# First FFN of a graph network in three parts: two early parts of 16 and 12 blocks beside the first attention, the rest behind it

## The chip, the cores and the metric

The kernel runs as one program on one core of a Trainium2 chip. The metric is the time of one execution on the device in microseconds (us); the median of ten executions is what is compared.

## The reference

6250 nodes with 256 features pass through four residual layers: graph attention, a routed FFN with eight experts, a weighted neighbour sum, and a second FFN whose experts are chosen by another graph attention. Both graphs' edges come with the inputs. What the change touches is the second layer, which needs the first:

```python
x = x + _L0_gnn_ref(_layernorm(x, axis=-1), edge_index, ...)      # graph attention, 206250 edges, 4 heads
x = x + _L0_ffn_ref(_layernorm(x, axis=-1)[None], ...)[0]         # routed FFN, below
x = x + _L1_gnn_ref(_layernorm(x, axis=-1), src, dst, edge_weight, ...)
x = x + _L1_ffn_ref(_layernorm(x, axis=-1)[None], ...)[0]

def _L0_ffn_ref(x, Wr, br, ln_g, ln_b, W1, b1, W2, b2):           # D = 256, E = 8 experts, H = 1024
    logits = xt @ Wr + br
    top_p, top_idx = jax.lax.top_k(jax.nn.softmax(logits), 2)
    weights = top_p / top_p.sum(axis=-1, keepdims=True)
    xn = layer norm of xt over its features
    xe = xn[None] * ln_g[:, None] + ln_b[:, None]
    h = jax.nn.gelu(jnp.einsum('end,edh->enh', xe, W1) + b1[:, None], approximate=False)
    y = jnp.einsum('enh,ehd->end', h, W2) + b2[:, None]
    out = (weights[:, :, None] * the two chosen rows of y).sum(axis=1)
```

A node's row of the FFN depends on its own row of the attention's output alone, so blocks of nodes can go through the FFN as soon as they are through the attention.

## The kernel before

The nodes, padded to 6272, are 49 blocks of 128. The edges, sorted by target, are 1612 tiles of 128, and 8 tiles (`Q`) make a piece; there are 202 pieces.

**First attention.** `gat_stream` (from L1497) runs one step per piece, in an order written out by hand (`manual_schedule`, L1722): instructions stand on each engine's queue in program order. Step `s_` has POOL issue 8 gathers of source rows (L1582, one for each tile), computes scores of the piece gathered one step earlier on VectorE, and adds the messages of the piece gathered seven steps earlier into PSUM on TensorE (L1691). The gathered rows have nine buffers. When a block's sums are complete, `done`, `normed`, `twice` and `logits` follow it, one of them per step, and write its normalized rows to a table in DRAM (L2223 for early blocks, L2225 for the others). `ends` (L2239) says after which blocks the two experts of a group of blocks are chosen; for early blocks a group has four blocks at most.

**The early part.** The first `EARLY` = 22 blocks belong to one `EarlyPart`. For each of its groups, a step apart: `chosen` (three parts of the ranking per step), `counted` (ranks inside the group, two matmuls, L789 and L790), `ranked` (places), and `put` (each block is loaded back from its table and scattered to its two experts' regions by POOL, L823). Behind the last group `tiles_of` (L833) turns the eight counts into a table of tiles of 256 rows, with two iotas on POOL; `filled` (L870) has SP read eight counts and write zeros behind each region (L876), and finds each token's place in the result and its gates. Then the part is `ready`.

The part's `beside` is a generator. The stream's steps call it five times each, and two of five calls return at once (L2251), so three slots a step remain. First come the expert parameters and the lists of the second graph, one after the other; then it waits for `ready` and goes into `run` (L898): after a start of four slots, every tile takes nine slots, with the tile's weights (`w`, three buffers of 1 MB, L922 and L927), its rows (L920) and its result (L983) on SP's queue, the first matmul at L953, the gelu at L959 and the second matmul at L975. `self.tiles` is the number of tiles that any routing could need, so the count doesn't depend on the data. When the stream's steps are over, whatever is left of the generator runs without them (L1790).

**The rest.** `head.ffn` calls `routed_ffn` (L494) for the other 27 blocks once the attention is complete. It ranks them on VectorE, finds the places with `2 * NT` small matmuls (L588), and runs tiles of 256 rows (`run_tiles`, L597): gathers of rows by POOL (L612), matmuls at L636 and L649, scatters of results (L652). `TT` tiles are the most that a routing can need; the last `n_exp // 2` = 4 of them stand behind a condition on the device (`more`, L548, and L674). After each tile it calls the generator `beside` `calls` times; with it comes `first.combined` (L988), which for each early block gathers the two results (L995), adds them to the block (L1008), and writes it and its normalized form to DRAM. The chunks of seven blocks at the end (L679) do the same for the rest.

```python
self.tiles = (2 * n * P + E0 * (TS - 1)) // TS           # L763, TS = 256, E0 = 8
TT = (2 * NP + n_exp * (TS - 1)) // TS                   # L505
TM = TT - n_exp // 2                                     # L514
nc.vector.tensor_scalar(more, end[:, n_exp - 1:], float(TM) + 0.5, None, op0=OP.is_gt)
```

The weighted sum (`weighted_sum`, L2288) reads the tables that both write, and starts behind them.

Of the kernel before, what the change touches and what calls it, by code (L numbers as in the profile page):

```python
# [20 lines left out]
F32 = mybir.dt.float32  # L21
BF = mybir.dt.bfloat16
I32 = mybir.dt.int32
I16 = mybir.dt.int16
AF = mybir.ActivationFunctionType
OP = mybir.AluOpType
# [6 lines left out]
P = 128  # L33
# [38 lines left out]
def tile_kernel(ctx, tc, src_ins, out):  # L72
    nc = tc.nc
# [680 lines left out]

    EARLY = 22

    class EarlyPart:


        def __init__(self, pool, head, n):  # L760
            TS = 2 * P
            self.head, self.n = head, n
            self.tiles = (2 * n * P + E0 * (TS - 1)) // TS  # L763
            self.cap = n * P + TS
            self.tab_x = dram.tile([n * P, D], F32, name="tab_xa")
            self.by_expert = dram.tile([E0 * self.cap, D], F32, name="xa_e")
            self.tab_y = dram.tile([self.tiles * TS, D], F32, name="tab_ya")
            self.inc = pool.tile([P, n, E0], F32, name="inca")
            self.g2 = pool.tile([P, n, 2], F32, name="g2a")
            self.place = pool.tile([P, 2, n], I32, name="placea")  # L770
            self.where = pool.tile([P, 2, self.tiles], I32, name="wherea")
            self.ready = False

        def begin(self, pool, ps):
            self.pool, self.ps = pool, ps
            self.count = pool.tile([P, E0], F32, name="counta")
            nc.vector.memset(self.count, 0.0)
            self.eo = pool.tile([P, E0], F32, name="eoa")
            nc.gpsimd.iota(self.eo, pattern=[[self.cap, E0]], base=0, channel_multiplier=0,
                           allow_small_or_imprecise_dtypes=True)  # L780
            self.zero = pool.tile([P, D], F32, name="zeroa")
            nc.vector.memset(self.zero, 0.0)

        def counted(self, t0, n, mp):
            sel, inc = self.head.sel[:, t0:t0 + n], self.inc[:, t0:t0 + n]
            nc.vector.tensor_copy(inc[:, 0], sel[:, 0])
            for t in range(1, n):
                nc.vector.tensor_add(inc[:, t], inc[:, t - 1], sel[:, t])
            nc.tensor.matmul(self.ps[:, 0], before, inc[:, n - 1], start=True, stop=True)  # L789
            nc.tensor.matmul(self.ps[:, 1], ones, inc[:, n - 1], start=True, stop=True)  # L790
            return self.ranked, (t0, n, mp)

        def places(self, dst, ranks_, start, n, mp):
            sel = self.head.sel[:, ranks_:ranks_ + n]
            r = mp.tile([P, n, E0], F32, name=f"rka{n}", bufs=1)
# [19 lines left out]
        def put(self, t0, n, mp, pi, j, xs):  # L815
# [4 lines left out]
            if len(xs) == 2 or j == n:  # L820
                i, x = xs.pop(0)
                for k in range(2):
                    st = nc.gpsimd.indirect_dma_start(  # L823
                        out=self.by_expert, out_offset=bass.IndirectOffsetOnAxis(ap=pi[:, k, i:i + 1], axis=0),
                        in_=x, in_offset=None, bounds_check=E0 * self.cap - 1, oob_is_err=False)
                    tc.declare_no_dep(st.ins, group="xa_e", reason="each token has two places of its own")
                    tc.add_to_no_dep_group("xa_e", st.ins)
            if j < n:
# [4 lines left out]
        def tiles_of(self, mp):  # L833
# [13 lines left out]
            nc.vector.tensor_add(zo, self.eo, self.count)  # L847
            tio = p.tile([P, TA], F32, name="tioa")
            nc.gpsimd.iota(tio, pattern=[[1, TA]], base=0, channel_multiplier=0, allow_small_or_imprecise_dtypes=True)
# [5 lines left out]
            wide = [P, TA, E0]  # L855
            w = p.tile(wide, F32, name="wa")
            nc.vector.tensor_tensor(w[:, :, :E0 - 1], tio[:, :, None].to_broadcast([P, TA, E0 - 1]),
                                    end[:, None, :E0 - 1].to_broadcast([P, TA, E0 - 1]), op=OP.is_ge)
            tb = p.tile([P, TA], F32, name="tbb")
            nc.vector.tensor_reduce(tb, w[:, :, :E0 - 1], AX.X, OP.add)  # L860
# [9 lines left out]
        def filled(self, mp, zo, base):  # L870
# [7 lines left out]
            r, pl = self.places(self.place, 0, base, n, self.pool)  # L878
            eq = self.pool.tile([P, n, E0], F32, name="eqa")
            for k in range(2):  # L880
                nc.vector.tensor_tensor(eq, r, pl[:, k, :, None].to_broadcast([P, n, E0]), op=OP.is_equal)
                nc.vector.tensor_mul(eq, eq, self.head.gates[:, :n])
                nc.vector.tensor_reduce(self.g2[:, :, k], eq, AX.X, OP.add)
            self.ready = True

        def beside(self, par, lists):
            for _ in par:
                yield True
            for part in lists:
                with tc.tile_pool(name="srt", bufs=1) as sp, tc.tile_pool(name="srt_ps", bufs=1, space=PSUM) as pp:  # L890
                    for _ in part(sp, pp):
                        yield True
            while not self.ready:
                yield True
            with tc.tile_pool(name="ffa", bufs=1) as fp, tc.tile_pool(name="ffa_ps", bufs=2, space=PSUM) as pp:
                yield from self.run(fp, pp)
# [90 lines left out]

        def combined(self, pool, x_d, x_e, tab_e):  # L988
            def load(b):
                x = pool.tile([P, 1, D], F32, name="xa")  # L990
                nc.sync.dma_start(x[:, 0], x_d[b * P:(b + 1) * P])
                ys = []
                for k in range(2):
                    y = pool.tile([P, D], F32, name=f"ya{k}")
                    nc.gpsimd.indirect_dma_start(  # L995
                        out=y, out_offset=None, in_=self.tab_y,
                        in_offset=bass.IndirectOffsetOnAxis(ap=self.place[:, k, b:b + 1], axis=0))
                    ys.append(y)
                return x, ys

            ahead = load(0)
            yield
            for b in range(self.n):
                x, ys = ahead
                if b + 1 < self.n:
                    ahead = load(b + 1)
                for k in range(2):
                    nc.vector.scalar_tensor_tensor(x[:, 0], ys[k], self.g2[:, b, k:k + 1], x[:, 0], op0=OP.mult, op1=OP.add)  # L1008
                nc.sync.dma_start(x_e[b * P:(b + 1) * P], x[:, 0])
                em = pool.tile([P, 1, D], F32, name="ema")  # L1010
                layernorm(pool, em, x, 1)
                nc.sync.dma_start(tab_e[b * P:(b + 1) * P], em[:, 0])
                yield

# [1124 lines left out]
    def fast(flag_s0, tab, NI, si, dl, il):  # L2139
# [18 lines left out]
        f0 = chosen_by.enter_context(tc.tile_pool(name="f0f", bufs=1))  # L2158
        NA = EARLY
        head = Head(f0, NA)  # L2160
        first = EarlyPart(f0, head, NA)
        with tc.tile_pool(name="gat0f", bufs=1) as g0:
# [57 lines left out]
            def logits(b, mp, xt, mv, sd, xT):  # L2220
                scaled(mp, xt, xt, mv, sd)
                if b < NA:
                    nc.sync.dma_start(first.tab_x[b * P:(b + 1) * P], xt)  # L2223
                else:
                    nc.sync.dma_start(head.tab_x[(b - NA) * P:(b + 1 - NA) * P], xt)  # L2225
                head.logits(mix[:, P + D:P + D + E0], xT, b)
                if b in ends:
                    t0 = max([e + 1 for e in ends if e < b], default=0)
                    n = b + 1 - t0
                    return chosen, (head.select(hp, t0, n), (t0, n) if b < NA else None, mp)  # L2230

            def chosen(parts, early_, mp):
# [3 lines left out]
                if early_ is not None:  # L2236
                    return first.counted, (*early_, mp)

            ends = tuple(min(NA, t + 4) - 1 for t in range(0, NA, 4)) + (NA + (NT - NA) // 2, NT - 6, NT - 1)  # L2239
            with tc.tile_pool(name="f0h", bufs=1) as hp, tc.tile_pool(name="mix_ps", bufs=1, space=PSUM) as xp:  # L2240
                mix = xp.tile([P, 4 * P], F32, name="mix")
                o = P + D + E0
                first.begin(hp, mix[:, o:o + 2 * E0].rearrange("p (k e) -> p k e", k=2))
                par = head.params(hp)
                side = first.beside(par, (lambda sp, pp: sorted_edges(s1, sp, pp, si1, dst1),
                                          lambda sp, pp: weights_of(s0, sp, pp, wt_d),
                                          lambda sp, pp: sorted_ends(s1, sp, pp, dst1, dl1, il1, flag1)))
                turn = itertools.count()

                def beside(flush=False):  # L2250
                    if not flush and next(turn) % 5 in (1, 3):  # L2251
                        return True
                    return next(side, None) is not None

# [27 lines left out]
        with tc.tile_pool(name="early", bufs=2) as yp:  # L2282
            head.ffn(f0, first.combined(yp, x_d, x_e, tab_e), combine, NA, calls=1)
        chosen_by.close()
# [310 lines left out]
```

## Time and profile before

| | us |
|---|---|
| median of 10 runs (6117.49 to 6136.03) | 6126.25 |
| profiled execution, its own time | 6122.44 |
| span of the profiled execution | 6120.7 |
| mean granted TensorE clock | 0.834 |
| first attention: first and last gather (L1582) | 122.6 and 2286.9 |
| lists of the second graph written (last L1935) | 1011.7 |
| early FFN: first and last start at L953 and L975 | 1404.2 and 2303.3 |
| rest of the FFN: first and last start at L636 and L649 | 2407.2 and 2929.3 |
| first gather of the weighted sum (L234) | 2988.2 |

The profile is of one execution. PE is TensorE's matmuls, PEld its weight loads, DVE VectorE, ACT ScalarE, POOL GpSimd, SP the queue that issues most transfers. A slice of the page is a fortieth of the span, 153 us, and a digit a tenth. In a timeline each row has its start and its duration in us, and in brackets the idle time before it and what ended it. The busy time of PE, DVE, ACT and POOL over the span is 4342.9, 3223.1, 1366.1 and 4100.7 us. A matmul of 32-bit floats shows as two records for each instruction, so a tile of the FFN has 32 records in each of its two layers.

### The profile page before, as it was taken

To read this page: it belongs to the slowest core of one execution; us is meant where nothing else is said; L and a number is where in the kernel's file an instruction comes from. 1 tells how busy PE (TensorE), PEld (TensorE's weight loads), DVE (VectorE), ACT (ScalarE), POOL (GpSimd) and SP (SyncE) were. 2 spreads that over 40 slices of the span, in tenths; PEclk is the share of its full clock that TensorE was granted. 3 is DMA by queue.
4 is the path that set the end of the run, shared out by engine and by line. 5 is a ranking of instruction groups with operands and counts; after the bars stand their busy time and mean duration, and the time that the engine had idled before them with its cause. 6 is when DMAs were issued, how large, how long until landed. Compare 5 with 4: busy or idle time off the path is not lost.

```text
span 6120.7 us, 67115 instructions
## 1 busy us (share of the span) xinstructions
PE 4342.9 (71%) x20648; PEld 3312.9 (54%) x20648; DVE 3223.1 (53%) x8690; ACT 1366.1 (22%) x3038; POOL 4100.7 (67%) x4311
## 2 busy tenths in 40 slices
PE   4466666658998997999478899999999997111111
PEld 3344544447777886787245666666666665111111
DVE  5788987656666675311422222222232224777777
ACT  2122111113333342422002222222222223000001
POOL 1777777777777771422377777777777757777774
PEclk8778777779999997999688999999999998555555
DMA  7545465547777774754534444444444433333332
GB/s 186 148 139 145 139 173 170 148 140 240 228 230 222 238 219 147 243 191 156 184 111 120 128 128 127 128 127 129 127 130 129 124 103 93 80 75 78 71 78 51
DMA packets 543876, 890.85 MB, mean 146 GB/s; under 512 B 146208, under 2 KB 384942, under 8 KB 543470
## 3 DMA queue, kind: packets, MB, share of 16 engines
q0 software_dynamic: 190688, 461.74, 28.2%
q1 hardware_dynamic: 333242, 406.39, 20.9%
q10 hardware_dynamic: 19572, 18.23, 0.9%
q8 instruction: 173, 2.83, 0.2%
q14 instruction: 201, 1.65, 0.1%
HBM read 784.77 MB, written 104.42 MB: 145 GB/s over the span
## 4 chain that ended last, share of the span: by engine, by line
PE 27%; POOL 10%; DVE 9%; issue 8%; DMA 5%; ACT 2%; DVEq 0%; SPq 0%; POOLq 0%; ACTq 0%
PE acc L2318 8%; POOL g L234 6%; PE pf L2028 5%; PE pf L2016 5%; POOL g L1582 4%; PE py L649 2%; DMA g<-tab_1f,si1s 2%; PE ph L636 2%; DMA g<-tab_ef,si 2%; PE pf L2026 2%; DVE xo L2116 1%; DVE oh L1458 1%; PE bacc L2334 1%; DVE s L1673 1%; DVE g L1675 1%
## 5 line engine op out<-in xcount | busy, mean ns | idle before, releaser
L1582 POOL DMA_INDIRECT g<-tab,si x1612 | 1578.6, 979 | 538.1 <-issue 490.3
L234 POOL DMA_INDIRECT g<-tab_ef,si x1612 | 1532.5, 951 | 547.4 <-issue 461.9
L2318 PE MATMUL acc<-g,oh 128*128 128x256 f32 x3224 | 867.1, 409 | 213.5 <-DMA g<-tab_ef,si 117.0
L1691 PE MATMUL acc<-g,oh 128*128 128x264 f32 x3224 | 913.7, 440 | 65.4 <-DVE g L1668 54.9
L1582 POOL DMA_INDIRECT g<-tab_1f,si1s x787 | 756.3, 961 | 245.5 <-issue 212.4
L2318 PEld LDWEIGHTS acc<-g,oh 128*128 128x128 f32 x3224 | 614.9, 201 | 451.6 <-issue 268.2
L1691 PEld LDWEIGHTS acc<-g,oh 128*128 128x128 f32 x3224 | 708.4, 223 | 223.8 <-DVE g L1668 70.7
L1668 DVE TENSOR_TENSOR g<-g,mix 128x2048 f32<-128x2048 f32 x202 | 459.6, 2275 | 59.7 <-ACT xT L2217 31.3
L2306 DVE TENSOR_SCALAR oh<-iota,dl,wt 128x128 f32<-128x128 f32 x1612 | 432.1, 362 | 87.8 <-PE acc L2318 83.9
L2016 PE MATMUL pf<-xt,w 128*128 128x512 f32 (+1 forms) x832 | 397.5, 610 | 55.1 <-ACT h L2021 55.1
L1603 PEld LDWEIGHTS <-ot 128*128 128x128 bf16 x2879 | 121.0, 101 | 509.0 <-issue 484.7
L2028 PE MATMUL pf<-w,h 128*128 128x256 f32 x1568 | 394.4, 395 | 0.0
L1691 PE MATMUL acc<-s,oh 128*128 128x72 bf16 x1267 | 91.1, 248 | 369.4 <-DVE s L1673 369.4
L2028 PEld LDWEIGHTS pf<-w,h 128*128 128x128 f32 x1568 | 283.9, 191 | 96.9 <-issue 65.7
L1691 PEld LDWEIGHTS <-oh 128*128 128x128 bf16 x1267 | 85.1, 131 | 377.3 <-issue 366.8
L953 PE MATMUL pf<-xe,w 128*128 128x256 f32 x928 | 231.6, 400 | 54.2 <-DVE xe L946 43.1
L2016 PEld LDWEIGHTS pf<-xt,w 128*128 128x128 f32 x832 | 158.1, 203 | 197.4 <-issue 118.8
L636 PE MATMUL ph<-xe,w 128*128 128x256 f32 x1088 | 248.6, 387 | 13.0 <-ACT h L639 13.0
L1458 DVE TENSOR_TENSOR oh<-zt,dl 128x1024 f32<-128x1024 f32 x202 | 244.5, 1211 | 0.0
L649 PE MATMUL py<-w,h 128*128 128x256 f32 x1088 | 243.8, 382 | 0.0
L636 PEld LDWEIGHTS ph<-xe,w 128*128 128x128 f32 x1088 | 210.7, 194 | 44.7 <-ACT h L639 15.3
L2376 DVE TENSOR_SCALAR ss<-ss 128x1 f32<-128x1 f32 x49 | 7.5, 154 | 418.1 <-ACT ss L2372 418.1
(548 smaller groups left out, 6424.6 us busy)
## 6 DMA issues: line engine op xcount, KB each, us to landing
w<-in_L_ffn_W SPq DMA_DIRECT2D x126, 1024.0 KB
db<-s_d SPq DMA_DIRECT2D x149, 512.0 KB
yb<-y_d SPq DMA_DIRECT2D x49, 640.0 KB
g<-tab,si POOLq DMA_INDIRECT x1612
g<-tab_ef,si POOLq DMA_INDIRECT x1612
y_d<-y SPq DMA_DIRECT2D x196, 128.0 KB
g<-tab_1f,si1s POOLq DMA_INDIRECT x787
bb<-in_L_ffn_b SPq DMA_DIRECT2D x63, 128.0 KB
```

The lines of the kernel that those rows point to most:

```text
L234: nc.gpsimd.indirect_dma_start(out=dst, out_offset=None, in_=table, in_offset=bass.IndirectOffsetOnAxis(ap=si[:, t:t + 1], axis=0))
L636: nc.tensor.matmul(ph, w1[:, k, f * P:(f + 1) * P], xe[:, k, :], start=(k == 0), stop=(k == KD - 1))
L649: nc.tensor.matmul(py, hs[f][:, i * P:(i + 1) * P], w2[:, f, :], start=(f == 0), stop=(f == FC - 1))
L953: nc.tensor.matmul(ph[:, f], w1[:, k, (f0_ + f) * P:(f0_ + f + 1) * P], xe[:, k], start=(k == 0), stop=(k == KD - 1))
L1458: nc.vector.tensor_tensor(o[:, :m], ips[:, None, k * P:(k + 1) * P].to_broadcast([P, m, P]), dl[:, a:a + m, None].to_broadcast([P, m, P]), ...
L1582: nc.gpsimd.indirect_dma_start(out=g[:, j, :DH + H], out_offset=None, in_=tab, in_offset=bass.IndirectOffsetOnAxis(ap=si[:, t0 + j:t0 + j ...
L1668: nc.vector.tensor_mul(gh, gh, ps[0][:, o:o + n, :, None].to_broadcast([P, n, H, CD]))
L1691: nc.tensor.matmul(acc[b].rearrange("p s w -> p (s w)"), oh[:, t - a], m_, start=(t == lo), stop=(t == hi))
L2016: nc.tensor.matmul(ph[:, :n], w1[:, e, k, f * P:(f + 1) * P], xts[g][:, k, :n], start=(k == 0), stop=(k == KD - 1))
L2028: nc.tensor.matmul(py[:, :D], hs[g, e, f][:, j * P:(j + 1) * P], w2[:, e, f, :], start=False, stop=(f == FC - 1))
L2306: nc.vector.tensor_scalar(oh[:, j], iota, dl[:, t0 + j:t0 + j + 1], wt[:, t0 + j:t0 + j + 1], op0=OP.is_equal, op1=OP.mult)
L2318: nc.tensor.matmul(acc[i], oh[:, t - t0], g[:, t - t0, :], start=(t == lo), stop=(t == hi))
```

## The change

`EARLY` becomes `(16, 12)`: two objects of `EarlyPart`, for blocks 0 to 15 and 16 to 27, each with tables, counts and tiles of its own. The ranking groups are those of each part (four blocks at most). The generator beside the stream runs parameters and lists as before, then part 1's tiles when part 1 is ready, then part 2's when part 2 is. The rest has 21 blocks. `combined` becomes one function that goes through the blocks of both parts, and `head.ffn` is asked for two calls of it after each tile. The two parts share the zeros that are written behind the regions, and some scratch tiles.

```diff
-    EARLY = 22
+    EARLY = (16, 12)
...
-        def __init__(self, pool, head, n):
+        def __init__(self, pool, head, t0, n):
             TS = 2 * P
-            self.head, self.n = head, n
+            self.head, self.t0, self.n, self.tag = head, t0, n, f"a{t0}"
             self.tiles = (2 * n * P + E0 * (TS - 1)) // TS
...
-        def beside(self, par, lists):
-            for _ in par:
-                yield True
-            for part in lists:
-                with tc.tile_pool(name="srt", bufs=1) as sp, tc.tile_pool(name="srt_ps", bufs=1, space=PSUM) as pp:
-                    for _ in part(sp, pp):
-                        yield True
+        def beside(self):
             while not self.ready:
                 yield True
-            with tc.tile_pool(name="ffa", bufs=1) as fp, tc.tile_pool(name="ffa_ps", bufs=2, space=PSUM) as pp:
+            with tc.tile_pool(name=f"ff{self.tag}", bufs=1) as fp, \
+                    tc.tile_pool(name=f"ff{self.tag}_ps", bufs=2, space=PSUM) as pp:
                 yield from self.run(fp, pp)
...
+    def combined(early, pool, x_d, x_e, tab_e):
+        todo = [(part, b) for part in early for b in range(part.n)]
+        ahead = todo[0][0].load(pool, x_d, 0)
+        yield
+        for i, (part, b) in enumerate(todo):
+            x, ys = ahead
+            if i + 1 < len(todo):
+                ahead = todo[i + 1][0].load(pool, x_d, todo[i + 1][1])
+            for k in range(2):
+                nc.vector.scalar_tensor_tensor(x[:, 0], ys[k], part.g2[:, b, k:k + 1], x[:, 0], op0=OP.mult, op1=OP.add)
...
-        NA = EARLY
+        NA = sum(EARLY)
         head = Head(f0, NA)
-        first = EarlyPart(f0, head, NA)
+        parts = [EarlyPart(f0, head, sum(EARLY[:i]), n) for i, n in enumerate(EARLY)]
+        part_of = [part for part in parts for _ in range(part.n)]
...
-            ends = tuple(min(NA, t + 4) - 1 for t in range(0, NA, 4)) + (NA + (NT - NA) // 2, NT - 6, NT - 1)
+            ends = tuple(part.t0 + min(part.n, t + 4) - 1 for part in parts for t in range(0, part.n, 4)) + (NA + (NT - NA) // 2, NT - 6, NT - 1)
...
+                def in_turn():
+                    yield from par
+                    for make in lists:
+                        with tc.tile_pool(name="srt", bufs=1) as sp, tc.tile_pool(name="srt_ps", bufs=1, space=PSUM) as pp:
+                            yield from make(sp, pp)
+                    for part in parts:
+                        yield from part.beside()
+
+                side = in_turn()
...
-            head.ffn(f0, first.combined(yp, x_d, x_e, tab_e), combine, NA, calls=1)
+            head.ffn(f0, combined(parts, yp, x_d, x_e, tab_e), combine, NA, calls=2)
```

## The prediction

> **What bounds the kernel now.** I read the slices of the page first, then busy time by stretch, then the queues of single engines where two stages meet. The slices show four stages: lists and first attention (up to slice 14), the rest of the first FFN (to 19), weighted sums, second attention. Only the first two are touched.
>
> ```profile
> PE   4466666658998997999478899999999997111111
> POOL 1777777777777771422377777777777757777774
> PEclk8778777779999997999688999999999998555555
> ```
>
> Slices 7 and 8 (1071 to 1377 us) have a half-idle TensorE. The stretches put numbers to it (columns: length, then busy time of PE, PEld, DVE, ACT, POOL with counts, granted clock, DMA share, GB/s):
>
> ```profile
> 1160.00:1397.00 237.00, 136.73 (x582) 104.44 (x581) 145.83 (x367) 34.91 (x88) 180.15 (x190) 0.76 0.52 148
> 1397.00:2303.50 906.50, 838.63 (x4459) 712.10 (x4458) 603.26 (x1190) 332.01 (x680) 651.56 (x680) 0.98 0.74 228
> 2303.50:2351.20 47.70, 33.24 (x142) 25.80 (x140) 38.39 (x85) 13.01 (x32) 0.00 (x0) 0.91 0.32 107
> ```
>
> Before 1397 nothing is near full by busy time, yet POOL is the bound, as its own timeline shows:
>
> ```profile
> 1105.29 0.94 POOL L1582 DMA_INDIRECT g<-tab,si  x1 [0.30 <-DMA g<-tab,si]
> 1106.54 0.95 POOL L1582 DMA_INDIRECT g<-tab,si  x1 [0.30 <-issue]
> 1107.79 1.02 POOL L823 DMA_INDIRECT xa_e<-xsa,pia  x1 [0.30 <-issue]
> 1109.11 1.01 POOL L823 DMA_INDIRECT xa_e<-xsa,pia  x1 [0.30 <-issue]
> ```
>
> A gather starts every 1.25 us, a scatter of the early part takes 1.32: the 0.30 between them is issue, never a wait. A step of the stream (8 gathers) cannot take under 10.0 us. From 1397 the early FFN runs beside it; 88 steps take 906.5 us, 10.30 each, with PE 93% and POOL (651.6 + 680 x 0.30) / 906.5 = 94% occupied. Two nearly full engines: FFN work beside the stream was almost free, and no room is left there. The FFN alone is PE-bound:
>
> ```profile
> 2784.98 7.07 PE L636 MATMUL ph<-xe,w 128*128 128x256 f32 x32
> 2791.89 0.60 PE L621 MATMUL pt<-ident,xg 128*128 128x128 f32 x4
> 2792.32 7.07 PE L649 MATMUL py<-w,h 128*128 128x256 f32 x32
> 2799.23 7.07 PE L636 MATMUL ph<-xe,w 128*128 128x256 f32 x32
> ```
>
> From L636 to L636 a tile takes 14.25 us.
>
> **How many tiles, and when.** The early part runs (2·n·128 + 8·255)//256 tiles: 29 for 22 blocks; 23 and 19 for 16 and 12, so 42. The rest has 34 before (L636 x1088, 32 records each); for 21 blocks 28, of which the last 4 stand behind a condition (needed > 24). The reference's routing on its own inputs gives blocks 28 to 48 (padding included) 670, 622, 755, 630, 872, 598, 543 and 686 rows per expert, 3+3+3+3+4+3+3+3 = 25 tiles, so the condition holds and all 28 run. In all 63 tiles become 70.
>
> Of five calls of beside per step the code skips two, and a tile has nine yields: 3 steps a tile, as the trace has it (906.5/29 = 31.3 us). Part 1 is ready when block 15 is: the scatters of blocks 12 to 15 end at 1122.8 (start 1121.80), and before, the last scatter (1359.67) came 37 us ahead of the first FFN load (1396.69). So part 1 starts near 1159, 237 us earlier, 22 steps of the loop (counted through its windows, step 92 in place of 114). Part 2's last block, 27, is ready 12 steps after its logits at step 129, long before part 1 ends. 23·9+4 and 19·9+4 slots are 128.7 steps: FFN from step 92 to 220. The last gather is issued in step 201, before's FFN ends in step 202, the loop in step 224. So 22 steps take 7 tiles in free PE time, 29 stand as before, and **6 tiles fall behind the last gather**, where nothing but the end of the stream covers them.
>
> **The sum**, against the profiled execution (6122.4 us, 6120.7 of it span; 3.9 under the median of 6126.25, so I add the change to the median).
>
> 1. Gathers. 24 scatters of blocks 16 to 27 now lie beside FFN (before, 12 of blocks 16 to 21 lay in POOL-bound steps without it). Steps 92 to 102: 11 x 10.30 = 113; 103 to 141: POOL 39 x 10.0 + 24 x 1.32 = 422; together 535 against 237 + 28 x 10.30 = 525 before: **+9**. Bounds: scatters hidden in 10.30 us steps, -11; added on top of them, +21.
>
> 2. Part 2's list (L833 to L884) is built in the middle of part 1's FFN. Before, its cover was the POOL-bound stretch:
>
> ```profile
> 1370.96 0.24 DVE L852 TENSOR_SCALAR tioa<-tioa,lasta 128x29 f32<-128x29 f32 x1 [19.45 <-POOL tioa L849]
> 1376.08 18.86 SPq L876 DMA_DIRECT2D xa_e<-zeroa  x8
> 1410.55 0.51 DVE L1592 TENSOR_SCALAR ot<-db,s_nid 128x1024 bf16<-128x1024 int16 x1 [7.83 <-DMA db<-s_d]
> 1404.19 3.60 PE L953 MATMUL pf<-xe,w 128*128 128x256 f32 x8 [2.52 <-DMA w<-in_L_ffn_W]
> ```
>
> VectorE stands 19.45 us on an iota that POOL has behind its gathers, then SP spends 18.86 on eight fills, with the stream's db loads (L1558) and the tiles' weights (L922, L927) queued behind; db came 7.83 and w 2.52 late. Those two are what a late SP cost, **+10**; bounds 0 (POOL lost one gap of 2.55) and 38 (both stalls passed on). The second start of an FFN waits for xg and w again, 1.01 + 2.52: **+4**, up to 14 (four empty slots). Three groups' counts (L789) now make an FFN-laden PE wait for inca (5.78 us at 487.69, 6.71 at 1298.34); POOL-bound steps hide most: **+5**, 0 to 18.
>
> 3. The end of the stream. PE has 33.2 us of work in 47.7, so 14 idle. Six tiles are 85.5; while sums still run (seven steps) they fill the idle time, after that each waits for xe (2.11 in the row at 1723.65), 4 x 2.1 = 8. 33 + 85.5 + 8 + 3 (ACT late, 1.59 at 1732.95, twice) = 130 against 48: **+82**. Bounds: all idle filled, +72; none, +98.
>
> 4. The rest: 6 tiles fewer, **-85.5**. Its place matmuls (L588) go from 108 to 84 records of 23.31 us: **-5**. Of the four closing chunks the six-block one goes, 2972.72 to 2981.34 between two em: **-9**.
>
> 5. Six more blocks are combined beside the rest. While 22 were, nine tiles took 2407.30 to 2556.94, 149.6 in place of 128.3: 0.97 a block, **+6**; 0 if hidden, +33 if two per tile (calls=2) double the loss of all 28.
>
> Sum: 9+10+4+5+82-85.5-5-9+6 = +16.5, **6143 us**. Without the cover of the gather queue, the 7 early tiles would cost 100 more.
>
> Thirteen more tiles beside the stream mean more function changes on ACT: L959's table loads are x41 of 1283 ns for 29 tiles, so some 18 more and as many back (the stream's own functions follow at L2199, x40), 36 x 1.283 = 46 us: nothing in the sum, since ACT is 37% busy there; 46 if that cover were gone. The Trainium skill (ScalarE: Activation LUTs, Table sets: the hidden batching unit) speaks against this change: it wants activations batched by table set and puts a switch at about 2.7 us there, though its section What ACT_TABLE_LOAD costs has 1283 ns as this trace does. By 2.7 us the 36 loads would be 97 us, an estimate from that page.
>
> **The rivals.**
>
> *The gather queue hides everything* (faster): scatters at -11, no stalls, the six tiles at +72, blocks hidden: -11+72-85.5-5-9 = -38.5, 6088. For it: idle PE of 100 us in 1160 to 1397; against: POOL is full once scatters join. It decides if part 2's list is built with POOL still never waiting. A half-way version lands near 6105.
>
> *A wash*: the scatters cost their 9, the stalls nothing: 9+82-85.5-5-9+6 = -2.5, 6124. For it: the stream absorbed the same stall before; against: it had an idle PE then.
>
> *SP and VectorE stall a full PE*: item 2 at its ends 38+14+18 and item 5 at 33: 9+70+82-85.5-5-9+33 = +94.5, 6221; half of that excess, 6180, is likelier. For it: SP is one queue; against: weights are asked for some 20 us ahead.
>
> *The condition doesn't hold* (the change then does more than it says): 4 tiles and PE's gap before them (10.91 at 2866.88) go, 4 x 14.25 + 10.91 = 68 off the forecast, 6075. Against: 25 against 24, no expert's rows near a multiple of 256 by less than 13.
>
> **How the numbers follow.** Forecast 0.48 (its own range 6128 to 6160), wash 0.24, all hidden 0.17, stalls 0.09, condition 0.02. 0.2% is 12 us, about what a measurement can tell: faster 0.17 + 0.02 = 0.19; same 0.24 + 0.06 of the forecast's lower edge = 0.30; slower 0.51. The range 6105 to 6182 leaves out most of the first and fourth rivals' far ends.
>
> **What would show it.** L953 starts near 1166, x1344 in all; L1582 ends near 2315 (before 2286.9), late by more if item 2 is too small; last L975 near 2460; L636 x896; L588 x84; about 36 more ACT table loads. I am wrong if the first attention's PE end moves by under 90 or over 130 us, or L636 counts 768.

## The result and the profile after

The changed kernel takes 6182.49 us (median of 8 runs, 6172.79 to 6188.48) against 6126.19 us of the kernel before in the same series: a ratio of 1.0088, 95% interval 1.0079 to 1.0097, or 56 us more. The forecast was 6143 us, 17 more, in a range of 6105 to 6182: the result lies at the range's upper end. The profiled execution has a span of 6179.0 us at a mean granted clock of 0.838, 58.3 us over that of the kernel before. Some of the series below ran where the kernel before itself took 7367 to 7457 us, so each ratio there is to the runs of the kernel before beside it, and a difference of times goes only with its own series.

The page's slices after, three lines that answer to those of before:

```profile
PE   4566666699888998789578999999999998111111
POOL 1777777777767670342277777777777766777774
PEclk8678777899999999899778999999999999555555
```

Slices are counted from 0, and are 154 us here. Part 1 begins late in slice 7, and slice 8 goes from 5 tenths of PE to 9: the half-idle stretch is filled. But slices 10 to 12 (1545 to 2008 us) read 8 throughout, where before reads 9, 9 and 8, and early tiles now reach to slice 16. In this document a step is named by the start of the first of its eight gathers on POOL (L1581, L1582 before); step 200 is the last full one. The lines of the kernel stand one to three lower than before, from L953 to L950 and from L975 to L972 in the early tiles. By stretch, after (length, then busy time of PE, PEld, DVE, ACT, POOL with counts, granted clock, DMA share, GB/s):

```profile
1166.00:1397.00 231.00, 210.24 (x1103) 177.98 (x1102) 156.36 (x354) 83.59 (x173) 170.94 (x179) 0.95 0.76 239
1397.00:1941.00 544.00, 477.35 (x2499) 402.20 (x2498) 353.35 (x751) 181.13 (x377) 399.70 (x417) 0.96 0.74 228
1969.30:2319.00 349.70, 312.97 (x1637) 262.56 (x1635) 225.51 (x459) 122.45 (x252) 245.00 (x256) 0.96 0.72 219
2319.00:2499.70 180.70, 157.75 (x731) 132.84 (x729) 74.96 (x192) 62.54 (x120) 11.91 (x15) 0.97 0.38 117
```

and two stretches of before that answer to the third and to the end of the stream, steps 168 to 200 and from there to the first tile of the rest:

```profile
1942.50:2273.10 330.60, 312.05 (x1661) 265.94 (x1662) 227.11 (x455) 123.85 (x253) 244.83 (x257) 0.98 0.76 236
2273.10:2407.30 134.20, 89.34 (x411) 76.68 (x411) 98.85 (x334) 29.03 (x61) 26.32 (x31) 0.76 0.32 97
```

The same 32 steps with the same early work take 349.70 us in place of 330.60. PE is busy for the same 312 us, with 36.7 us idle in place of 18.6, and at a lower clock, 0.96 for 0.98. The waits of PE say for what (us in total, times, longest), in this stretch after:

```profile
PE pf L950 <- DVE xe L943: 31.7, 11, 6.4
PE pf L950 <- ACT h L956: 3.0, 5, 0.6
```

and before:

```profile
PE pf L953 <- DVE xe L946: 16.3, 11, 3.2
PE pf L953 <- ACT h L959: 2.0, 3, 1.6
```

As often as before, but twice as long in total, PE waits for a tile's scaled input, xe. Along the whole path of the two profiled executions, the 57.7 us by which the weighted sum's first gather comes later (3045.9 against 2988.2) are made of: 3.9 up to step 138; **15.6** in steps 138 to 150, where part 2's list is made (six scatters of its last blocks, L825, stand there too); 7.5 in steps 162 to 168, where part 2's tiles begin; **19.1** in steps 168 to 200; **96.1** from step 200 to the first tile of the rest (230.3 against 134.2); then -75.2 for the rest with its 28 tiles (446.9 against 522.1) and -9.2 for what closes it (49.7 against 58.9).

The list's stall shows in three rows of after, VectorE's wait for an iota, SP's fills and the late db, a load of edge targets that VectorE compares with the nodes' numbers (ot):

```profile
1679.80 0.23 DVE L854 TENSOR_SCALAR tioa<-tioa,lasta 128x19 f32<-128x19 f32 x1 [11.40 <-POOL tioa L851]
1690.27 20.98 SPq L878 DMA_DIRECT2D x_ea<-zeroa  x8
1723.20 0.48 DVE L1591 TENSOR_SCALAR ot<-db,s_nid 128x1024 bf16<-128x1024 int16 x1 [13.73 <-DMA db<-s_d]
```

A late VectorE holds up PE. Its waits for nd, the nodes' part of the scores, which VectorE sums, in steps 138 to 150 of after and then of before:

```profile
PE pd L1602 <- DVE nd L1611: 10.3, 4, 4.5
```

```profile
PE pd L1603 <- DVE nd L1612: 2.3, 1, 2.3
```

POOL then waits 7.5 us for PE's sums in these steps of after (0.3 before), and neither PE nor VectorE has a wait for a gathered row among its listed ones there: nothing shows POOL with its scatters to be what holds these steps up.

The groups confirm the counts (busy us, mean ns, idle before):

```profile
L950 PE MATMUL pf<-xe,w 128*128 128x256 f32 x1344 | 346.9, 409 | 105.9 <-DVE xe L943 90.2 <-ACT h L956 12.3 <-DMA w<-in_L_ffn_W 3.4
L636 PE MATMUL ph<-xe,w 128*128 128x256 f32 x896 | 205.5, 387 | 18.8 <-ACT h L639 18.8
L588 PE MATMUL pl_ps<-qo,ro 128*128 128x56 f32 x84 | 18.2, 420 | 12.5 <-DVE ro L584 12.5
L956 ACT ACT_TABLE_LOAD x58 | 74.4, 1283 | 3.2 <-PE pf L950 2.3
```

1344 / 32 = 42 early tiles and 896 / 32 = 28 behind, so the condition on the device held.

### The profile page after: what moved, and what is told of

Read it like the earlier page. It is cut to its first block, busy times and chain, and to the rows that moved or that the text cites. A ratio compares the mean times of both kernels' runs of the same rounds, so it can differ in the third digit from the quotient of the medians.

```text
span 6179.0 us, 68440 instructions
## 1 busy us (share of the span) xinstructions
PE 4431.4 (72%) x21104; PEld 3389.0 (55%) x21104; DVE 3245.3 (53%) x8784; ACT 1428.4 (23%) x3133; POOL 4105.3 (66%) x4314
## 4 chain that ended last, share of the span: by engine, by line
PE 38%; POOL 19%; DVE 15%; issue 13%; DMA 11%; ACT 4%; DVEq 0%; SPq 0%; ACTq 0%; POOLq 0%
POOL g L1581 13%; PE acc L2331 8%; POOL g L234 6%; PE pf L2027 5%; PE acc L1690 5%; PE pf L2015 4%; PE pf L950 3%; DMA g<-tab,si 3%; PE pf L972 3%; DMA g<-tab_1f,si1s 2%; DMA g<-tab_ef,si 2%; DVE oh L1457 2%; PE pf L2025 2%; DVE g L1667 2%; PE ph L636 1%
## 5 line engine op out<-in xcount | busy, mean ns | idle before, releaser
L1581 POOL DMA_INDIRECT g<-tab,si x1612 | 1581.3, 981 | 564.5 <-issue 493.3
L1690 PE MATMUL acc<-g,oh 128*128 128x264 f32 x3224 | 890.2, 430 | 48.9 <-DVE g L1667 38.2
L1581 POOL DMA_INDIRECT g<-tab_1f,si1s x787 | 756.0, 961 | 245.8 <-issue 211.5
L950 PE MATMUL pf<-xe,w 128*128 128x256 f32 x1344 | 346.9, 409 | 105.9 <-DVE xe L943 90.2
L2027 PE MATMUL pf<-w,h 128*128 128x256 f32 x1568 | 394.4, 395 | 0.0
L950 PEld LDWEIGHTS pf<-xe,w 128*128 128x128 f32 x1344 | 262.5, 203 | 163.5 <-DVE xe L943 108.0
L2027 PEld LDWEIGHTS pf<-w,h 128*128 128x128 f32 x1568 | 283.9, 191 | 96.9 <-issue 65.7
L972 PE MATMUL pf<-w,h 128*128 128x256 f32 x1344 | 318.7, 386 | 9.3 <-ACT h L956 9.3
L972 PEld LDWEIGHTS pf<-w,h 128*128 128x128 f32 x1344 | 253.8, 192 | 46.7 <-ACT h L956 12.8
L1457 DVE TENSOR_TENSOR oh<-zt,dl 128x1024 f32<-128x1024 f32 x202 | 244.6, 1211 | 0.0
L1602 PE MATMUL pd<-nbw,ot 128*128 128x24 bf16 x1612 | 71.1, 174 | 223.6 <-DVE nd L1611 188.4
```

The lines of the kernel that those rows point to most:

```text
L950: nc.tensor.matmul(ph[:, f], w1[:, k, (f0_ + f) * P:(f0_ + f + 1) * P], xe[:, k], start=(k == 0), stop=(k == KD - 1))
L972: nc.tensor.matmul(py[:, i], hs[f][:, i * P:(i + 1) * P], w2_[:, f], start=(f == 0), stop=(f == FC - 1))
L1457: nc.vector.tensor_tensor(o[:, :m], ips[:, None, k * P:(k + 1) * P].to_broadcast([P, m, P]), dl[:, a:a + m, None].to_broadcast([P, m, P]), ...
L1581: nc.gpsimd.indirect_dma_start(out=g[:, j, :DH + H], out_offset=None, in_=tab, in_offset=bass.IndirectOffsetOnAxis(ap=si[:, t0 + j:t0 + j ...
L1602: nc.tensor.matmul(pd[:, j].rearrange("p s d -> p (s d)"), o[:, i * P:(i + 1) * P], nbw[b] if s.group else NB[:, b].rearrange("p s d -> p ...
L1690: nc.tensor.matmul(acc[b].rearrange("p s w -> p (s w)"), oh[:, t - a], m_, start=(t == lo), stop=(t == hi))
```

## A theory: the slot at which part 2 begins

A step has three slots for early work: at its head, in its middle and at its end. A tile takes nine, three steps, so every tile of a part stands in its steps exactly as the part's first tile does. Part 1 takes 23·9 + 4 = 211 slots, and 211 = 3·70 + 1: part 2 begins one slot later in the step than part 1. Part 1's tiles are transposed at the end of a step and scaled at the head of the next one; part 2's are transposed at the head and scaled in the middle. What lies between on VectorE is seen in the tile of part 2 that is transposed at 2000 us of after, in VectorE's timeline (start, duration, operation, in brackets the wait before it):

```profile
2000.66 0.29 DVE L1639 TENSOR_TENSOR d<-zt,M 128x128 f32<-128x128 f32 x1
2000.87 0.74 DVE L979 TENSOR_TENSOR y<-pf,bb 128x256 f32<-128x256 f32 x2
2001.54 0.15 DVE L2177 SCALAR_TENSOR_TENSOR rd<-bacc,po 128x4 f32<-128x4 f32 x1
...
2003.62 0.42 DVE L2188 SCALAR_TENSOR_TENSOR hs<-o,hs 128x256 f32<-128x256 f32 x1
2004.08 0.43 DVE L2195 BATCH_NORM_STATS2 bs<-hs 128x6 f32<-128x256 f32 x1
...
2006.83 0.29 DVE L1656 TENSOR_TENSOR pw<-zt,il 128x128 f32<-128x128 f32 x1 [1.74 <-ACT pw L1654]
2007.04 1.22 DVE L1457 TENSOR_TENSOR oh<-zt,dl 128x1024 f32<-128x1024 f32 x1
2008.17 0.99 DVE L943 TENSOR_SCALAR xe<-pf,pa 128x256 f32<-128x256 f32 x2
```

and what PE does meanwhile:

```profile
2000.48 0.60 PE L936 MATMUL pf<-ident,xg 128*128 128x128 f32 x4
...
2001.28 1.06 PE L1690 MATMUL acc<-g,oh 128*128 128x264 f32 x4
2008.76 3.78 PE L950 MATMUL pf<-xe,w 128*128 128x256 f32 x8 [6.42 <-DVE xe L943]
2012.33 3.22 PE L1690 MATMUL acc<-g,oh 128*128 128x264 f32 x12
```

The transposes are done at 2001.1. VectorE then closes a block of nodes (L2177 to L2197), waits 1.74 us for ACT, makes the one-hots (L1457, the matrices with which PE adds messages to their nodes), and only then scales: PE waits 6.42 us. And its next eight records take 3.78 us, where such a group takes 1.9 to 2.0 elsewhere.

**Theory A:** this place in the step costs the 19 us of steps 168 to 200, the 7.5 of the start and some 20 of the end of the stream. **Rival B:** VectorE and SP are too full beside the second part's tiles, wherever they begin. **Rival C:** it is part 2's list, by its fills and its iotas. **Rival D:** the code for several parts or the two calls of `combined` cost by themselves.

## The experiments

**Part 2 one slot earlier.** Its start of four slots becomes three, and part 2 then begins 210 slots after part 1.

```diff
-            for _ in range(4):
+            for _ in range(4 if self.t0 == 0 else 3):
                 yield True
```

> Part 2's FFN waits three slots at its start where the changed kernel waits four, so its transposes come at the same point of a step of the stream as part 1's. Theory 'place in the step': part 2's TensorE waited 2.3 to 3.3 us per tile for xe because the transposes stand at the start of a step and xe behind the one-hots on VectorE; with part 1's place the steps 162 to 201 go from 10.77 us towards 10.1 and the time falls by 20 to 30, to about 6155. Rival 'full engines': those steps are slow because PE, POOL and the transfers are all nearly full; one slot fewer is worth 2 us, 6180.

> The same kernel as slot3, because on the chip of that call the kernel before took 7447 us with transfers that landed tens of us late, and after itself was not beside it. Expected where the kernel before takes about 6126: theory 'place in the step' 6150 to 6162, rival 'full engines' 6180.

> Part 2's feed-forward begins one step of the stream earlier, so that its tiles stand in the steps as part 1's do. Theory (the place of a tile in the step costs the 19 us in the stream and some 20 us of the tail): 0.003 to 0.007 below the changed kernel's ratio of this series (15 to 45 us). Rival (part 2's tiles wait because VectorE is full, wherever they begin): the changed kernel's ratio within 0.002.

The first two gave 1.0061 (1.0040 to 1.0082) of a kernel before of 7447 us, and 1.0087 (1.0056 to 1.0118) of one of 7367 us, without the changed kernel beside them, so they settle nothing about it. The third ran beside the changed kernel itself, which had its own expectation:

> The changed kernel itself, beside the other kernels of this series. It took 1.0088 of the kernel before where that one takes 6126 us; two kernels of it were since run where the kernel before takes 7370 to 7450 us, and gave 1.0061 and 1.0087 (part 2 one step earlier) and 1.0147 and 1.0156 (part 2's list spread out). Theory: all that the change adds is waits of TensorE, which grow with the time of the whole, so that it takes 1.009 to 1.012. Rival: the waits of TensorE come from engines that are themselves held up where the kernel takes 7400 us, and it takes 1.014 to 1.018.

In that series the kernel before took 6127.12 us, the changed kernel 6179.27 (1.0085, 1.0068 to 1.0102) and this one 6134.98 (1.0012, 1.0002 to 1.0021). One slot is worth **44 us** of the 52 that the change costs there: a ratio lower by 0.0073, at the upper end of theory A's 0.003 to 0.007 and far from rival B's 0.002, and more than the 20 to 30 us expected at first. What the control was to say of a 7400 us kernel before is left open. The profiled run of the kernel with one slot earlier took 6127.24 us, 8 under its median, so its stages show a little more than those 44. The same tile in this run, PE and then VectorE:

```profile
1990.12 0.60 PE L936 MATMUL pf<-ident,xg 128*128 128x128 f32 x4
1992.83 2.02 PE L950 MATMUL pf<-xe,w 128*128 128x256 f32 x8 [2.11 <-DVE xe L943]
```

```profile
1992.03 0.29 DVE L1639 TENSOR_TENSOR d<-zt,M 128x128 f32<-128x128 f32 x1
1992.24 0.99 DVE L943 TENSOR_SCALAR xe<-pf,pa 128x256 f32<-128x256 f32 x2
1993.14 0.15 DVE L2177 SCALAR_TENSOR_TENSOR rd<-bacc,po 128x4 f32<-128x4 f32 x1
```

xe now stands ahead of the block of nodes, and the wait is 2.11 us. Over steps 168 to 200 PE's waits for xe are again what they were before:

```profile
PE pf L950 <- DVE xe L943: 16.2, 11, 3.2
```

Its stretches, steps 168 to 200 and the early tiles behind them:

```profile
1959.10:2284.80 325.70, 308.74 (x1667) 263.63 (x1668) 229.55 (x471) 125.20 (x256) 244.78 (x257) 0.99 0.77 239
2284.80:2446.50 161.70, 148.29 (x695) 125.69 (x693) 70.01 (x179) 60.12 (x115) 11.77 (x15) 0.98 0.40 126
```

24.0 us less in the first and 19.0 in the second, as theory A has it, at a clock of 0.99; steps 162 to 168 take 63.9 us in place of 70.2. Rival B falls: VectorE has as much to do (229.55 us in place of 225.51), and the waits for it are down to those of the kernel before. Steps 138 to 150 still take 143.4 us (126.1 before): the list's cost is another matter.

**The same place in the kernel before.** One slot more at the start of its only part.

```diff
-            for _ in range(4):
+            for _ in range(5):
                 yield True
```

> The kernel before with five waiting slots at the start of its early FFN in place of four, so all of its 29 tiles get the place in the step that part 2 has in the changed kernel. Theory 'place in the step': 29 tiles lose 1 to 2 us each, less what the gather queue hides: 25 to 45 us slower, 6150 to 6170. Rival 'full engines': one slot is worth 2 us, 6128.

It took 1.0119 (1.0078 to 1.0159) of a kernel before of 7447 us. So the place costs without a second part too, and more than the 25 to 45 us of theory A: some 89 us of 7447. The rival's 2 us lie outside the interval. Its steps 168 to 200:

```profile
2306.60:2754.90 448.30, 335.93 (x1646) 276.35 (x1645) 225.58 (x450) 124.22 (x253) 244.94 (x257) 0.87 0.58 172
```

against those of the next experiment, in the same series, with the first tile's slot where the kernel before has it:

```profile
2286.70:2706.20 419.50, 332.77 (x1653) 280.24 (x1654) 226.29 (x450) 124.28 (x253) 245.08 (x257) 0.89 0.60 186
```

In the eight profiles of the series where the kernel before takes 7367 us and more, these 32 steps take 409.0 to 419.5 us in the five whose tiles there have the slot of the kernel before, and 442.2 to 454.5 in the three that have the other.

**The new code with one part.** The changed kernel with one part of 22 blocks and two calls after each tile.

```diff
-    EARLY = (16, 12)
+    EARLY = (22,)
```

> The changed kernel's code with one part of 22 blocks, two calls of combined per tile kept: the kernel before but for the new functions and the calls. If code and calls cost nothing: 6126, within 5. Rival 'two per tile': the tiles of the rest that run beside combined lose twice as much, 6145 to 6155.

1.0000 (0.9975 to 1.0024). Rival D falls: its 6145 to 6155, a ratio of 1.003 to 1.005, lies outside the interval, and the code and the two calls cost nothing that can be measured here.

**Part 2's list spread out.** Both iotas are made when the part is set up, and of part 2's eight fills SP gets one in each step.

```diff
+            self.tio = pool.tile([P, TA], F32, name=f"tioa{self.t0}")
...
-            tio = p.tile([P, TA], F32, name=f"tioa{self.t0}")
+            tio = self.tio
...
-        def filled(self, mp, zo, base):
+        def filled(self, mp, zo, base, k=0):
...
+                if k + m < E0:
+                    return self.filled, (mp, zo, base, k + m)
```

> The changed kernel with the two iotas of each part's table made at the start, and part 2's eight zero fills spread over eight steps, one in each. Theory 'late list': in the changed kernel the steps 138 to 150 lost 15.6 us against before, since VectorE stood 11.40 on the iota and then 13.73 on a db load behind 20.98 us of fills; without them 12 to 16 less, about 6168. Rival: the steps lost that to the 24 scatters on POOL, and the time stays within 4 of 6182.

> The same kernel as lists, for the same reason. Expected where the kernel before takes about 6126: theory 'late list' 6166 to 6170, rival 6178 to 6186.

1.0147 (1.0109 to 1.0185) and 1.0156 (1.0107 to 1.0205). The changed kernel was not run beside them, so a gain over it can't be read. Steps 138 to 150 took 164.3 and 174.2 us, against 175.3 and 174.0 with one slot earlier in the same two series: one gain and one none. The experiment is inconclusive, and nothing speaks for rival C as the main cause. Its part 2 begins at the changed kernel's slot, which goes with ratios 0.007 to 0.009 above those of the kernel with one slot earlier in the same two series.

**Fewer blocks in part 2.** Parts of 16 and 6: as many early blocks as before, 36 early tiles in place of 29, and 34 behind them as before. One call after each tile.

```diff
-    EARLY = (16, 12)
+    EARLY = (16, 6)
...
-            head.ffn(f0, combined(parts, yp, x_d, x_e, tab_e), combine, NA, calls=2)
+            head.ffn(f0, combined(parts, yp, x_d, x_e, tab_e), combine, NA, calls=1)
```

> Two early parts of 16 and 6 blocks: as many blocks early as the kernel before has in one part, so 36 early tiles and 34 behind, and their last tile beside the last gathers and not 100 us behind them. Theory (what the change costs is tiles that stand behind the last gather; a second part itself costs under 30 us, and saves the 78 us that the kernel before has behind its last gather): 0.988 to 0.996 of the kernel before. Rival (a second part costs its list, its start and its place in the step whatever its size, and the tail stays): 1.002 to 1.008.

6172.66 us, 1.0077 (1.0060 to 1.0094), where the rival had it (1.002 to 1.008): my theory of it was wrong twice. The 78 us that I took for early tiles behind the last gather of the kernel before are mostly the stream's own: its last L975 ends at 2303.6, 30 us behind step 200, so there was little to save. And part 2 begins at the same bad slot. Its stretches are those of the changed kernel, and then nearly those of before:

```profile
1953.10:2304.20 351.10, 313.44 (x1650) 263.00 (x1647) 225.39 (x444) 123.30 (x252) 244.84 (x256) 0.97 0.72 218
2304.20:2449.60 145.40, 98.51 (x442) 84.08 (x441) 102.78 (x347) 30.47 (x64) 26.41 (x31) 0.76 0.31 95
```

Steps 168 to 200 take 20.5 us more than before here, with nearly all early tiles beside the stream, and what is behind step 200 takes 11.2 more. So it is the place, more than the seven tiles that a second part adds by its rounding, that seems dear; parts of 16 and 6 at the other slot were not run. Here the second list is made in steps 113 to 117, and the cost goes with it: steps 138 to 150, with neither list nor scatter, take 126.1 us as before, and steps 108 to 120 take 130.1, where the changed kernel, with no list there, takes 121.6.

**The wait taken away in another manner.** The next tile's transposes come before this tile's second product, and its scaling beside that product, in all early tiles of the changed kernel.

```diff
+            def turned(xg):
...
+            def scaled(pt, pa):
...
-                    if f0_ == 2 and j + 1 < self.tiles:
+                    if f0_ == 0 and j + 1 < self.tiles:
                         now = start(j + 1)
...
+                if j + 1 < self.tiles:
+                    pt = turned(now[2])
...
+                            xe = scaled(pt, now[1])
```

> The changed kernel with the next tile's transposes before this tile's second product and its scaling (xe) beside that product, in all of the early feed-forward. Theory (TensorE's waits for xe, 9 us in 100 of part 2 and some 8 in 100 of the tail, and 4 in 100 of part 1, are what a tile costs more than 14.4 us): the waits go, part 2 keeps up with the stream, the last early matmul is 30 to 60 us earlier, and the ratio is 0.004 to 0.008 below the changed kernel's. Rival (the waits move to the next thing that VectorE makes late, the one-hots or the turned inputs, and TensorE is no faster): the changed kernel's ratio within 0.002.

6153.31 us, 1.0046 (1.0029 to 1.0063): 26 us less than the changed kernel, a little under what was expected. No wait for xe is left in steps 168 to 200, which take 323.5 us, and the early tiles behind them take 161.7, as with one slot earlier. But steps 92 to 138, in part 1, take 511.2 us in place of the control's 493.4, with a new wait there:

```profile
PE pf L985 <- ACT h L966: 34.2, 6, 8.2
```

The rival is right for part 1, where the old order's longest wait for xe was 3.2 us and the new one makes the gelu late, and the theory for part 2.

**Parts of 12 and 16, and of 14 and 14.** Both begin each part at part 1's slot of the changed kernel, by a counter of slots. The edit of the first; the second has `(14, 14)`.

```diff
-    EARLY = (16, 12)
+    EARLY = (12, 16)
...
-            for _ in range(4):
+            for _ in range(3):
+                yield True
+            while self.head.turn % 3 != 0:
                 yield True
...
+                    head.turn += 1
                     return next(side, 0) != 0
```

> Two early parts of 12 and 16 blocks, 42 early tiles as in the changed kernel, each part begun at the slot of the step at which part 1 begins in the changed kernel. Part 1's list and the sorted lists before it end 10 steps earlier, so its tiles begin at step 84 and not 94 and the last early tile ends 8 steps earlier; part 2's list falls into three steps between the two parts with no tile beside them. Theory (with the place in the step mended, a tile costs its time only where it stands behind the last gather, some 8 us a step there, and what begins earlier lies under the gather queue): 45 to 75 us under the kernel with part 2 one step earlier (1.0012 of the kernel before), so 0.989 to 0.994. Rival (the steps before 94 have no idle time that a tile could use, or the end of the stream takes its time whatever stands there): 0.999 to 1.004.

> Two early parts of 14 and 14 blocks, 42 early tiles, both begun at that slot; they follow without a gap, and the last early tile ends 2 steps earlier than with 12 and 16, 10 earlier than in the changed kernel, but part 2's list is made beside part 1's tiles, as there. Theory (the list costs 15 to 17 us where tiles stand beside it, and little in a gap): its ratio is 0.000 to 0.002 above that of 12 and 16, 0.990 to 0.995, and steps 138 to 150 take 140 us and more. Rival (the list costs the same in the gap): 0.002 to 0.003 below that of 12 and 16.

They took 0.9994 (0.9972 to 1.0016) and 1.0010 (0.9988 to 1.0032) of a kernel before of 7457 us. Against the kernel before the first missed its 0.989 to 0.994 and lies where the rival had it (0.999 to 1.004), and the second missed its 0.990 to 0.995. Against the kernel with one slot earlier, which ran in other series (7447 and 7367 us for the kernel before), the first is lower by 0.0067 and 0.0093, or 50 and 69 us, within its theory's 45 to 75; from step 200 to the rest it takes 179.1 us, in place of 227.6 and 222.2. So an earlier first part does take tiles from behind the last gather, and over the kernel before no gain is shown. How 12 and 16 does where the kernel before takes 6127 us was not tried. Steps 138 to 150, with the list made between the parts (12 and 16) and beside part 1's tiles (14 and 14):

```profile
1939.00:2092.50 153.50, 113.62 (x543) 93.08 (x543) 87.61 (x181) 40.88 (x84) 98.68 (x104) 0.85 0.62 190
```

```profile
1962.60:2127.70 165.10, 120.63 (x577) 99.22 (x577) 88.96 (x186) 43.35 (x89) 94.07 (x101) 0.84 0.59 183
```

11.6 us apart, on the side that was expected (part of it is that fewer tiles stand in that stretch with 12 and 16); with one part of 22 and no list there it was 157.2. The two kernels' ratios, 0.0016 apart, have overlapping intervals.

## Why the prediction was right in its sign and wrong in its size

The sign is right, and most terms are near. The time, 39 us over the forecast and outside its own range of 6128 to 6160, came out at the wide range's upper end, next to the 6180 that the third rival was given as its likelier value. Both are luck: that rival's time is made of SP's stalls and of two calls that double a loss, and the runs show neither at that size.

1. *Gathers and counts* (+9 and +5): 3.9 us up to step 138, between the forecast and the lower bounds: most of it lies under POOL's queue.
2. *Part 2's list* (+10): 15.6 us in the profiled execution, 18.9 in the control. The rows fit the mechanism named, SP's fills and a late db: db came 13.73 us late and not 7.83, with tiles on PE this time, which waited 10.3 us for nd in place of 2.3. That the fills and not the iota made it so is not shown. *The second start* (+4): 7.5, of which all but 1.2 was gone with one slot earlier. It was no wait for xg and w, but the first tile's xe (a wait of 7.97 us at 1939.08).
3. **The step that failed** is the count of tiles: "a tile has nine yields: 3 steps a tile", "29 stand as before". The 211 slots were in the working, but only as a length; which slot of the step part 2 gets by them was not asked. The runs show that this slot costs 44 us. Nothing in the sum, and no rival, has the 19.1 us of steps 168 to 200. Rival 3 had a full PE made to wait, but by SP and the load of VectorE, which the slot alone refutes.
4. *The end of the stream* (+82, with -5 for the place matmuls behind it, +77 to the first tile of the rest): +96.1. With one slot earlier it is 211.8 us, +77.6: the term was right for tiles at the place of before, and the excess, 18.5, is the slot's again. The wait for xe was priced by a row of before, 2.11 us, which holds for the other slot.
5. *The rest* (-85.5, +6 for the blocks combined): -75.2, 4 short of the -79.5; *the last chunk* (-9): -9.2.
6. *The table loads*, nothing in the sum: 58 in place of 41, near the 18 more that were counted, and 33 more in the whole kernel (407 against 374) where some 36 were named. The load at 2005.06 takes 1.28 us and the next activation starts at 2006.35, so the page's 2.7 us for a switch is not seen here. ACT stays free enough, though one of them stands in the chain of waits at the bad slot (ACT loads a table at 2005.06, pw is late, then the one-hots, then xe).

Of the signs named beforehand, L950 starts at 1170.1 (1166 forecast), and its count, L636's and L588's are as forecast; the last gather comes at 2333.3 and not near 2315, the last L972 at 2499.4 and not near 2460, and TensorE's end of the first attention moves by 148.5 us (2351.2 to 2499.7), beyond the 130 that were to show me wrong.

The errors have opposite signs. With the slot mended the change costs 8 us (1 to 13 by the interval), under the forecast of 17; its profile reaches step 138 2.9 us ahead of the kernel before, where the sum had 14 more for gathers and counts, so the gather queue seems to hide more than I allowed. The slot adds 44.

## What to carry to other kernels

Where work is dealt out to slots of a loop written by hand, its place in the loop's body is as much a part of the change as its amount: count the slots modulo the body's own, and look at what the next engine has between the producer and the consumer at the new place. A row of before gives the price of a wait only for that place. And a wait of TensorE is to be priced with the slow clock that can follow it, as the next section has it.

## What the hardware showed that I had not expected

How long TensorE stands idle, and when, decides how fast it runs afterwards. In six traces (before, after, the control, the third with one slot earlier, 16 and 6, and the transposes ahead) I took each group of eight records of L950 or its like that begins behind a wait of 0.6 us or more: of 105 with a wait under 1.5 us none was slow (1.99 to 2.02 us for the eight); of 69 with 1.5 to 2.2 us, 16 were slow, over 2.4 us; of 14 with 2.2 to 3.0, 9; of 50 with 3.0 and more, 49, and the median of these 50 is 3.60. The granted clock in the row of after's wait of 6.42 us and in that of one slot earlier with 2.11 us:

```profile
2008.76:2012.33 3.57, 3.57 (x8) 2.82 (x9) 3.47 (x7) 0.00 (x0) 0.90 (x1) 0.50 0.96 371
```

```profile
1992.83:1995.79 2.96, 2.96 (x15) 2.47 (x15) 2.75 (x9) 0.00 (x0) 2.35 (x3) 1.00 0.38 105
```

Half the clock for these 3.57 us, and for eight records that take 2.0 at full speed, so some 1.6 us are lost on top of the wait. In steps 168 to 200, 5 waits for xe of 3.0 us and more stand in after and 1 with one slot earlier; with the waits themselves, 31.7 against 16.2 us, 15.5 + 4 × 1.6 = 21.9 of the 24.0 us are accounted for, by this estimate.

The Trainium skill (TensorE: Matmul & The Clock Gate, What's actually happening) has this rule: the clock halves after an idle window of about 3.4 us and comes back after a busy one of the same length, in windows that run freely. The traces agree with the half clock and with the free windows: between 1150 and 2550 us of each of the six, changes of the granted clock lie whole multiples of 3.413 us apart, wherever the waits begin. So it matters how a wait falls on this grid. In after, 1.98 us of a wait of 2.36 us (it ends at 2301.8) lie in one window, and the next has half the clock:

```profile
2299.82:2303.23 3.41, 1.41 (x6) 1.17 (x7) 3.31 (x9) 0.33 (x2) 2.74 (x3) 1.00 0.75 198
2303.23:2306.65 3.42, 3.42 (x9) 2.69 (x8) 2.13 (x1) 2.28 (x4) 2.57 (x3) 0.50 0.95 308
```

With parts of 16 and 6 a longer wait, 3.25 us up to 1960.57, is cut in two by the grid, and the eight records behind it take 2.01 us at full clock:

```profile
1955.83:1959.24 3.41, 1.49 (x7) 0.94 (x5) 3.24 (x12) 0.64 (x2) 2.61 (x3) 1.00 0.82 176
1959.24:1962.66 3.42, 2.09 (x10) 1.75 (x11) 3.32 (x8) 0.98 (x2) 2.70 (x3) 1.00 0.77 215
```

Where the traces differ from the rule, they decide: a window need not be idle throughout. In these stretches there are 2146 windows at full clock. The next one was at half clock after all 115 in which PE was busy for under 42% of the time, after 17 of the 104 with 42 to 61%, and after none of the 1927 with more.
